# Sixteen-bit index rows for layer 1 of a four-layer graph network

## The chip, the cores and the metric

The kernel runs on one core of a Trainium2 chip. The metric is the device time of one execution in microseconds (us), given as the median over several executions. The profile is one further execution, recorded by the hardware profiler.

The engines are named as in the profile: PE multiplies matrices (PEld is its weight load), DVE is the vector engine, ACT the scalar engine, POOL the GpSimd engine, and SP the engine that issues most of the DMAs. A "q" behind a name (SPq, PEq) is that engine's instruction queue. Each engine runs its instructions in the order of its own queue, and waits on semaphores for the others.

## The reference

There are 12500 nodes with 32 features and 400000 edges. `src` is random and `dst` is sorted. Four graph layers follow each other, each with a residual and a layer norm:

```python
edge_index = jnp.stack([src, dst])
x = _layernorm(x + _L0_gnn_ref(x, edge_index, edge_weight1, edge_attr_3, edge_attr_5, L0_gnn_W), axis=-1)
x = _layernorm(x + _L1_gnn_ref(x, edge_attr_2, L1_gnn_weight, edge_index), axis=-1)
x = _layernorm(x + _L2_gnn_ref(x, edge_index, edge_attr_2, ...), axis=-1)
x = _layernorm(x + _L3_gnn_ref(x, edge_weight, edge_attr_3, edge_index, ...), axis=-1)
```

The change touches layer 1 alone. There the features are gathered at `edge_index[1]` (dst, sorted) and summed at `edge_index[0]` (src, random):

```python
def _L1_gnn_ref(x, edge_attr, weight, edge_index):   # weight: 4 x 4 x 32 x 32
    bu = _tent_basis(edge_attr[:, 0], k1)            # 4 hat functions each
    bv = _tent_basis(edge_attr[:, 1], k2)
    basis = (bu[:, :, None] * bv[:, None, :]).reshape(-1, k1 * k2)
    xj = x[edge_index[1]]
    w2 = weight.reshape(k1 * k2, f_in, f_out)
    msg = basis[:, 0:1] * (xj @ w2[0])
    for k in range(1, k1 * k2):
        msg = msg + basis[:, k:k + 1] * (xj @ w2[k])
    return jax.ops.segment_sum(msg, edge_index[0], num_segments=n_nodes)
```

## The kernel before

The edges are cut into tiles of 128. Five tiles (T = 5) make a group of 640 edges (SE), 25 groups (G) make a turn, and there are 25 turns (NG). Each layer is a hardware loop of five bodies, and each body holds five turns written out (U = 5), which is 125 groups. So a layer has 625 groups. Between two bodies all engines meet at a barrier.

The kernel is written in a framework that puts in the semaphores itself and also decides, when the program is built, in which order each engine gets its instructions. A planner walks through the program with a cost of its own for each instruction and each transfer, and gives an engine what is ready by that reckoning, the earlier in the source first. The order on an engine is therefore not always that of the source, and it is fixed before the program runs.

**The prologue** (L110 to L202) computes index tables. For layer 1 it loads `dst` as `t_i` (L169, 125 partitions of 25 x 128 integers), finds the even node below each tile's lowest target (`even`, L173 to L176), subtracts it (`rel_p`, L179) and writes the difference as 32-bit floats to the DRAM array `rel_d` (L182). Then it writes `mw_d` (L187) and reads it back as a row (`mw_row`, L189), from which two flags follow (L191 to L195). The pool that holds these tiles is given back after that, and the following constants (L260 on) use its space.

**Layer 1** (`turn1`, L685) works on a table `y_d` that holds, for every pair of nodes, the products with all 16 weight matrices. A group does this:

- SP loads four things: `bas` (L702, the 16 basis values of 640 edges, each spread over 8 partitions), `rel` (L709, the 640 differences of `rel_d`, the same row in all 128 partitions), five pieces of the table `yw` (L726, their addresses come from a register that SP loads), and `row` (L744, the 640 source indices, again the same row in all partitions). `bas`, `rel` and `row` have three buffers each.
- ACT copies `rel` into PSUM as `rel_p` (L711). This PSUM tile has one buffer.
- DVE compares `rel_p` with the node number that a partition stands for and multiplies by `bas`, in two halves `bm[:, h]` (L714).
- PE multiplies `bm` with `yw` into `pe` (L732), and ACT copies this out as `msg` (L740).
- DVE compares `row` with the sources along the partitions (`same`, L746), finds duplicates (`dup`, `later`, `to_f`, L750 to L756) and computes the rows to write to (`to`, L758).
- PE multiplies `msg` with `same` into `pm` (L762), which sums edges that share a source, and ACT copies this out as `add` (L764). `add` and `to` have four buffers.
- POOL issues five indirect DMAs (L766) which add the rows of `add` to five arrays `sums` in DRAM, at the rows in `to`.

The other layers (L0, L2, L3: `edge_pass`, L328) gather with indirect DMAs on POOL and add in SBUF. They do not use `rel_d` or the source rows.

Of the kernel before, what the change touches and what calls it, by code (L numbers as in the profile page):

```python
# [9 lines left out]

F32 = mybir.dt.float32
I32 = mybir.dt.int32
AF = mybir.ActivationFunctionType
ALU = mybir.AluOpType
AX = mybir.AxisListType
# [5 lines left out]
P = 128  # L21
F = 32
T = 5
# [16 lines left out]
def kernel(  # L40
# [25 lines left out]
    nc = tc.nc  # L66
    N = x_in.shape[0]
# [8 lines left out]
    dram = ctx.enter_context(tc.tile_pool(name="dram", bufs=1, space=DRAM))  # L76
# [81 lines left out]
    NT = NG * GT  # L158
    NM = N // 2
    PT, RT = split(NT)  # L160
    rel_d = dram.tile([NT * P], F32, name="rel_d")
    pair_d = dram.tile([NT], I32, name="pair_d")
    over_i = const.tile([1, 1], I32, name="over_i")
    more_i = const.tile([1, NG], I32, name="more_i")
# [1 line left out]
    with tc.tile_pool(name="pre1", bufs=1) as pre:  # L166
        mw_d = dram.tile([NT], F32, name="mw_d")
        t_i = pre.tile([PT, RT, P], I32, name="t_i")
        nc.sync.dma_start(t_i, dst_n.rearrange("(q r e) -> q r e", r=RT, e=P))  # L169
        pair = pre.tile([PT, RT], I32, name="pair")  # L170
        even = pre.tile([PT, RT], I32, name="even")
        top = pre.tile([PT, RT], I32, name="top")
        nc.vector.tensor_reduce(even, t_i, AX.X, ALU.min)  # L173
        nc.vector.tensor_reduce(top, t_i, AX.X, ALU.max)
        nc.vector.tensor_scalar(pair, even, 1, None, op0=ALU.logical_shift_right)
        nc.vector.tensor_scalar(even, pair, 1, None, op0=ALU.logical_shift_left)  # L176
        nc.sync.dma_start(pair_d.rearrange("(q r) -> q r", r=RT), pair)
        rel_p = pre.tile([PT, RT, P], F32, name="rel_p")
        nc.vector.tensor_tensor(  # L179
            rel_p, t_i, even[:, :, None].to_broadcast([PT, RT, P]), ALU.subtract  # L180
        )
        nc.sync.dma_start(rel_d.rearrange("(q r e) -> q r e", r=RT, e=P), rel_p)  # L182
        nc.vector.tensor_tensor(top, top, even, ALU.subtract)
        nc.vector.tensor_scalar(top, top, int(math.log2(V)), None, op0=ALU.logical_shift_right)
        mw = pre.tile([PT, RT], F32, name="mw")
        nc.vector.tensor_copy(mw, top)
        nc.sync.dma_start(mw_d.rearrange("(q r) -> q r", r=RT), mw)  # L187
        mw_row = pre.tile([1, NG, GT], F32, name="mw_row")
        nc.sync.dma_start(mw_row, mw_d.rearrange("(a n g) -> a n g", a=1, g=GT))  # L189
        more = pre.tile([1, NG], F32, name="more")  # L190
        nc.vector.tensor_reduce(more, mw_row, AX.X, ALU.max)  # L191
        over = pre.tile([1, 1], F32, name="over")
        nc.vector.tensor_reduce(over, more, AX.X, ALU.max)
        nc.vector.tensor_scalar(over_i, over, 1.0, None, op0=ALU.min)
        nc.vector.tensor_scalar(more_i, more, 1.0, None, op0=ALU.max)  # L195
        pid = pre.tile([P, 1], I32, name="pid")
        nc.gpsimd.iota(pid, pattern=[[0, 1]], base=0, channel_multiplier=1)
        nc.vector.tensor_scalar(pid, pid, 4, None, op0=ALU.logical_shift_right)
        for h in range(2):
            nc.vector.tensor_scalar(  # L200
                nid[:, h : h + 1], pid, 2.0, float(h), op0=ALU.mult, op1=ALU.add
            )  # L202
# [352 lines left out]
    with ExitStack() as sums_es:  # L555
      acc0 = sums_of(sums_es, 0, 124, 2)
      with ExitStack() as es:
        pools = layer_pools(es, 0)
        io, work = pools[:2]
# [113 lines left out]
    with ExitStack() as es:  # L673
        io = es.enter_context(tc.tile_pool(name="io1", bufs=2))
        one = es.enter_context(tc.tile_pool(name="one1", bufs=1))
        work = es.enter_context(tc.tile_pool(name="work1", bufs=2))
# [8 lines left out]
        def turn1(i, pairs, ids):  # L685
            src_f = ps_s.tile([P, G, T], F32, name="src_f")
            nc.vector.tensor_copy(
                src_f.rearrange("p g t -> p (g t)"), src_all[:, ds(i, 1), :].rearrange("p a g -> p (a g)")
            )
            spare = io.tile([P, G, T], F32, name="spare")  # L690
            nc.vector.tensor_tensor(
                spare, past[:, None, :].to_broadcast([P, G, T]), src_f, ALU.subtract
            )
            for s in range(G):
                e0 = i * (G * SE) + s * SE

                def spread(of):
                    return of[ds(e0, SE)].rearrange("(a e) -> a e", a=1).to_broadcast([P, SE])


                bas = work.tile([P, T, P], F32, name="bas", bufs=3)
                nc.sync.dma_start(  # L702
                    bas,
                    basis_d[ds(i, 1), :, s * T : (s + 1) * T, :]
                    .rearrange("a k t e -> a k (t e)")
                    .to_broadcast([8, 16, SE]),
                )
                rel = work.tile([P, T, P], F32, name="rel", bufs=3)
                nc.sync.dma_start(rel.rearrange("p t e -> p (t e)"), spread(rel_d))  # L709
                rel_p = ps_r.tile([P, T, P], F32, name="rel_p")  # L710
                nc.scalar.copy(rel_p, rel)  # L711
                bm = work.tile([P, 2, T, P], F32, name="bm")
                for h in range(2):
                    nc.vector.scalar_tensor_tensor(  # L714
                        bm[:, h], rel_p, ids[:, h : h + 1], bas, op0=ALU.is_equal, op1=ALU.mult
                    )
                yw = work.tile([P, T, 2 * F], F32, name="yw", bufs=4)
                for t in range(T):
                    at = nc.values_load(
                        pairs[0:1, s * T + t : s * T + t + 1],  # L720
                        engines=[SP],
                        min_val=0,
                        max_val=NM,
                        skip_runtime_bounds_check_because="a target's pair or N / 2, by a min below",
                    )
                    nc.sync.dma_start(  # L726
                        yw[:, t, :], y_d[ds(at, 8)].rearrange("m k f -> (m k) f")
                    )
                pe = ps_e.tile([P, T, F], F32, name="pe")
                for t in range(T):  # L730
                    for h in range(2):
                        nc.tensor.matmul(  # L732
                            pe[:, t, :],
                            bm[:, h, t, :],
                            yw[:, t, h * F : (h + 1) * F],
                            start=(h == 0),
                            stop=(h == 1),
                        )
                msg = work.tile([P, T, F], F32, name="msg", bufs=3)
                nc.scalar.copy(msg, pe)  # L740


                row = work.tile([P, T, P], I32, name="row", bufs=3)
                nc.sync.dma_start(row.rearrange("p t e -> p (t e)"), spread(src_n))  # L744
                same = work.tile([P, T, P], F32, name="same", bufs=3)
                nc.vector.tensor_tensor(  # L746
                    same, row, src_f[:, s, :, None].to_broadcast([P, T, P]), ALU.is_equal
                )
                dup = work.tile([P, T, P], F32, name="dup")
                nc.vector.tensor_tensor(  # L750
                    dup, same, before_p[:, None, :].to_broadcast([P, T, P]), ALU.mult
                )
                later = work.tile([P, T], F32, name="later")
                nc.vector.tensor_reduce(later, dup, AX.X, ALU.max)
                to_f = work.tile([P, T], F32, name="to_f")
                nc.vector.tensor_tensor(to_f, later, spare[:, s, :], ALU.mult)  # L756
                to = work.tile([P, T], I32, name="to", bufs=4)
                nc.vector.tensor_tensor(to, to_f, src_f[:, s, :], ALU.add)  # L758

                pm = ps_m.tile([P, T, F], F32, name="pm")  # L760
                for t in range(T):
                    nc.tensor.matmul(pm[:, t, :], same[:, t, :], msg[:, t, :], start=True, stop=True)  # L762
                add = work.tile([P, T, F], F32, name="add", bufs=4)
                nc.scalar.copy(add, pm)  # L764
                for t in range(T):
                    nc.gpsimd.indirect_dma_start(  # L766
                        out=sums[t],
                        out_offset=bass.IndirectOffsetOnAxis(ap=to[:, t : t + 1], axis=0),
                        in_=add[:, t, :],
                        in_offset=None,  # L770
                        compute_op=ALU.add,
                    )
# [36 lines left out]
    with ExitStack() as sums_es:  # L809
      acc2 = sums_of(sums_es, 2, 97, 1)  # L810
      with ExitStack() as es:
        pools = layer_pools(es, 2)
        io, work = pools[:2]
# [43 lines left out]
    with ExitStack() as sums_es:  # L857
      acc3 = sums_of(sums_es, 3, 80, 1)
      with ExitStack() as es:
        pools = layer_pools(es, 3, agg_bufs=1, x_bufs=0)  # L860
        io, work = pools[:2]
# [251 lines left out]
```

## Time and profile before

| what | value |
|---|---|
| median of 3 runs | 20443.71 us (20440.81 to 20443.82) |
| the profiled execution | 20448.74 us, span 20447.0 us |
| layer 1, first load to last scatter | 4483.4 to 10598.6 us of the span |
| in 4484 to 10590 us: PE, DVE, ACT, POOL busy | 4390.8, 2690.6, 739.4, 4855.7 of 6106.0 us |
| DMA in the same stretch | 16 engines busy 0.70 of the time, 127 GB/s |
| loads of a group | `bas`, `rel`, `row` 320 KB each, `yw` five of 32 KB |
| granted PE clock in layer 1 | 0.50 |

How to read it. A line of the timeline has the start in us, the duration in us, the engine, the source line, the operation, "output <- input", how many instructions were merged (x), and in brackets how long the engine had been idle and what released it. A line of the waits has who waited for whom, the total in us, the number of times and the longest. "issue" means that the engine waited for nothing that the profile shows.

### The profile page before, as it was taken

What the parts mean: (1) busy time and instruction counts of PE and PEld (TensorE: products, weight loads), DVE (VectorE), ACT (ScalarE), POOL (GpSimd) and SP (SyncE); (2) the same over time, 40 slices, a digit from 0 to 9 for tenths busy, and PEclk for the clock granted to TensorE, in tenths of its full rate; (3) what the DMA queues carried; (4) which work ended last, traced back from release to release, by engine and by line L of the source; (5) the groups of instructions that cost most, each with busy time, mean ns of one, the idle gap of its engine ahead of it and who ended that gap; (6) DMA issues with size and microseconds to landing.
All of it is one profiled execution on the core that took longest, in us unless ns stands there. A gap on an engine that the chain in (4) does not pass through costs nothing. (4 is left out here: it accounts for less than half of the span.)

```text
span 20447.0 us, 197484 instructions
## 1 busy us (share of the span) xinstructions
PE 12719.0 (62%) x51816; PEld 9979.2 (49%) x51817; DVE 10310.0 (50%) x18014; ACT 3851.0 (19%) x9168; POOL 13886.4 (68%) x12511
## 2 busy tenths in 40 slices
PE   5676676777767676776752222222467676767676
PEld 5666666656666666666652222222423333333333
DVE  3333333324444444444442222222289999999998
ACT  0000000011111111111100000000044444444443
POOL 5777777718878787887867777777555555555554
PEclk9555555555555555555555555555566666666665
DMA  1111111137767676776750000000011111111111
GB/s 39 24 25 24 23 25 24 22 104 129 129 123 129 122 129 119 132 129 122 129 106 14 15 14 14 15 13 14 10 36 31 32 31 32 31 31 32 30 31 26
DMA packets 1764667, 1156.67 MB, mean 57 GB/s; under 512 B 1103399, under 2 KB 1511663, under 8 KB 1758192
## 3 DMA queue, kind: packets, MB, share of 16 engines
q1 hardware_dynamic: 1013443, 937.43, 18.4%
q0 software_dynamic: 750000, 205.60, 11.4%
q8 instruction: 441, 7.23, 0.2%
q14 instruction: 783, 6.41, 0.1%
HBM read 1024.87 MB, written 116.94 MB: 56 GB/s over the span
## 5 line engine op out<-in xcount | busy, mean ns | idle before, releaser
L354 POOL DMA_INDIRECT xg<-x,src x6250 | 6014.2, 962 | 3691.3 <-issue 1418.3
L378 PE MATMUL agg<-hot,prod 128*124 128x64 f32 (+1 forms) x18750 | 3871.3, 399 | 3939.0 <-DVE prod L843 2822.9
L766 POOL DMA_INDIRECT sums<-add,to x3125 | 4863.0, 1556 | 1620.8 <-issue 1073.4
L378 PEld LDWEIGHTS agg<-hot,prod 128*124 128x124 f32 (+1 forms) x18750 | 3687.1, 309 | 4125.4 <-issue 4048.9
L732 PE MATMUL pe<-yw,bm 128*128 128x32 f32 x12500 | 2926.0, 403 | 1452.5 <-DVE bm L714 1349.0
L959 PE MATMUL pr<-wr,h 64*128 64x512 f32 x6250 | 3128.9, 1030 | 1104.7 <-ACT pr L954 1042.2
L354 POOL DMA_INDIRECT xg<-in_x_in,src x3125 | 3007.8, 962 | 1064.1 <-issue 810.4
L732 PEld LDWEIGHTS pe<-yw,bm 128*128 128x128 f32 x12500 | 2757.9, 329 | 1622.1 <-DVE bm L714 1489.5
L714 DVE SCALAR_TENSOR_TENSOR bm<-rel_p,nid,bas 128x640 f32<-128x640 f32 x1250 | 1090.1, 881 | 3250.8 <-ACT rel_p L711 3245.6
L959 PEld LDWEIGHTS pr<-wr,h 64*128 64x128 f32 x6250 | 1078.3, 305 | 2511.0 <-ACT pr L954 1578.8
L396 DVE TENSOR_TENSOR acc<-acc,agg 124x128 f32 (+2 forms) x1875 | 446.8, 238 | 3190.2 <-PE agg L378 3181.8
L974 DVE TENSOR_TENSOR big<-pr,fa 128x1024 f32<-128x1024 f32 x1875 | 1845.7, 1039 | 396.7 <-ACT fa L946 395.5
L954 ACT COPY pr<-b2r 128x1024 f32<-128x1024 f32 x1875 | 1594.1, 872 | 1011.8 <-DVE big L974 991.7
L985 DVE TENSOR_REDUCE red<-big 128x160 f32<-128x2560 f32 x625 | 1756.9, 2811 | 0.0
L403 ACT COPY xp<-xg 128x160 f32<-128x160 f32 x1250 | 370.0, 296 | 7272.1 <-DMA xg<-x,src 3659.9
L762 PE MATMUL pm<-msg,same 128*128 128x32 f32 x6250 | 1464.7, 403 | 272.0 <-ACT msg L740 272.0
L762 PEld LDWEIGHTS pm<-msg,same 128*128 128x128 f32 x6250 | 1380.5, 329 | 356.2 <-ACT msg L740 356.2
L843 DVE TENSOR_TENSOR prod<-gauss,xp 128x480 f32<-128x480 f32 x625 | 408.5, 654 | 1775.5 <-ACT xp L403 1749.9
L378 PEld LDWEIGHTS agg<-hot,msg 128*80 128x80 f32 x6250 | 685.2, 199 | 1260.5 <-issue 670.9
L378 PE MATMUL agg<-hot,msg 128*80 128x64 f32 x6250 | 768.9, 290 | 532.0 <-DVE acc L396 438.5
L366 DVE TENSOR_TENSOR hot<-consts,rel 128x320 f32<-128x320 f32 x1875 | 901.8, 483 | 0.0
L740 ACT COPY msg<-pe 128x160 f32<-128x160 f32 x625 | 182.5, 292 | 3734.7 <-PE pe L732 3734.7
(167 smaller groups left out, 7558.3 us busy)
## 6 DMA issues: line engine op xcount, KB each, us to landing
bas<-basis_d SPq DMA_DIRECT2D x625, 320.0 KB
rel<-rel_d SPq DMA_DIRECT2D x625, 320.0 KB
row<-in_src_n SPq DMA_DIRECT2D x625, 320.0 KB
yw<-y_d SPq DMA_DIRECT2D x3125, 32.0 KB
xg<-x,src POOLq DMA_INDIRECT x6250
dist<-in_ew_n SPq DMA_DIRECT2D x625, 96.0 KB
xg<-in_x_in,src POOLq DMA_INDIRECT x3125
sums<-add,to POOLq DMA_INDIRECT x3125
```

What stands on the lines that cost most here:

```text
L354: nc.gpsimd.indirect_dma_start(out=xg[:, t, :], out_offset=None, in_=x_dram[layer], in_offset=bass.IndirectOffsetOnAxis(ap=src[:, s * T + ...
L366: nc.vector.tensor_tensor(hot, iota_w[:, None, :].to_broadcast([P, T, W]), begun[1][:, s, :, None].to_broadcast([P, T, W]), ALU.is_equal,)
L378: nc.tensor.matmul(agg[:, c, :], prod[:, t, a:b], hot[:, t, :], start=(t == 0), stop=(t == T - 1),)
L396: nc.vector.tensor_tensor(cols, cols, agg, ALU.add)
L714: nc.vector.scalar_tensor_tensor(bm[:, h], rel_p, ids[:, h : h + 1], bas, op0=ALU.is_equal, op1=ALU.mult)
L732: nc.tensor.matmul(pe[:, t, :], bm[:, h, t, :], yw[:, t, h * F : (h + 1) * F], start=(h == 0), stop=(h == 1),)
L762: nc.tensor.matmul(pm[:, t, :], same[:, t, :], msg[:, t, :], start=True, stop=True)
L766: nc.gpsimd.indirect_dma_start(out=sums[t], out_offset=bass.IndirectOffsetOnAxis(ap=to[:, t : t + 1], axis=0), in_=add[:, t, :], in_offset ...
L954: nc.scalar.copy(pr[:, : b - a, :], b2r.rearrange("p o u j -> p (o u j)")[:, None, :].to_broadcast([P, b - a, 512]),)
L959: nc.tensor.matmul(pr[:, k, :], h[64 * k : 64 * k + 64, a // 2, :], wr[64 * k : 64 * k + 64].rearrange("h o u j -> h (o u j)"), start=Fals ...
L974: nc.vector.tensor_tensor(big[:, a * 4 : b * 4], pr[:, : b - a, :].rearrange("p t (o u j) -> p (t o) u j", u=8, j=16), fa[:, a * 4 : b * 4 ...
L985: nc.vector.tensor_reduce(red.rearrange("p t o u -> p (t o) u"), big, AX.X, ALU.add)
```

## The change

`rel_d` becomes an array of 16-bit integers. A second array of 16-bit integers, `src_d`, is added. The prologue fills it: it loads `src` (125 partitions), converts it on DVE and writes it to DRAM. In layer 1 the tiles `rel` and `row` become 16-bit integers and are loaded from the two arrays, so that each of these loads has 160 KB in place of 320 KB. `rel_p` in PSUM, `same` and everything behind them stay 32-bit floats. No loop, buffer count or instruction of layer 1 is added or removed.

```diff
-    rel_d = dram.tile([NT * P], F32, name="rel_d")
+    assert N < 1 << 15
+    rel_d = dram.tile([NT * P], I16, name="rel_d")
+    src_d = dram.tile([NT * P], I16, name="src_d")
...
-        rel_p = pre.tile([PT, RT, P], F32, name="rel_p")
+        rel_p = pre.tile([PT, RT, P], I16, name="rel_p")
         nc.vector.tensor_tensor(
             rel_p, t_i, even[:, :, None].to_broadcast([PT, RT, P]), ALU.subtract
         )
         nc.sync.dma_start(rel_d.rearrange("(q r e) -> q r e", r=RT, e=P), rel_p)
+        s_i = pre.tile([PT, RT, P], I32, name="s_i")
+        nc.sync.dma_start(s_i, src_n.rearrange("(q r e) -> q r e", r=RT, e=P))
+        s_h = pre.tile([PT, RT, P], I16, name="s_h")
+        nc.vector.tensor_copy(s_h, s_i)
+        nc.sync.dma_start(src_d.rearrange("(q r e) -> q r e", r=RT, e=P), s_h)
...
-                rel = work.tile([P, T, P], F32, name="rel", bufs=3)
+                rel = work.tile([P, T, P], I16, name="rel", bufs=3)
                 nc.sync.dma_start(rel.rearrange("p t e -> p (t e)"), spread(rel_d))
                 rel_p = ps_r.tile([P, T, P], F32, name="rel_p")
                 nc.scalar.copy(rel_p, rel)
...
-                row = work.tile([P, T, P], I32, name="row", bufs=3)
-                nc.sync.dma_start(row.rearrange("p t e -> p (t e)"), spread(src_n))
+                row = work.tile([P, T, P], I16, name="row", bufs=3)
+                nc.sync.dma_start(row.rearrange("p t e -> p (t e)"), spread(src_d))
                 same = work.tile([P, T, P], F32, name="same", bufs=3)
                 nc.vector.tensor_tensor(
                     same, row, src_f[:, s, :, None].to_broadcast([P, T, P]), ALU.is_equal
```

More of the change, by code (lines that the diff above doesn't have):

```diff
@@ L12 @@
 I32 = mybir.dt.int32
+I16 = mybir.dt.int16
 AF = mybir.ActivationFunctionType
```

## The prediction

> **What bounds layer 1 now.** I read first the windows over layer 1: no engine is full (POOL 4855.7 of 6106 us, PE 4390.8, DMA 0.70). So something goes round. The waits of layer 1 (who, for whom, total us, times, longest) say who waits in every group:
>
> ```profile
> ACT msg L740 <- PE pe L732: 3734.7, 625, 6.1
> DVE bm L714 <- ACT rel_p L711: 3245.6, 624, 7.9
> POOL sums L766 <- issue: 1072.2, 2961, 2.6
> ACT add L764 <- DMA sums<-add,to: 761.5, 313, 2.4
> ACT add L764 <- PE pm L762: 759.1, 312, 2.4
> ...
> ACT rel_p L711 <- DMA yw<-y_d: 94.4, 4, 26.0
> ```
>
> No wait for `rel`, `row` or `bas` comes 625 times: the loads are on time. DVE waits for ACT's copy `rel_p`, ACT for PE. The timeline of one group shows the ring:
>
> ```profile
> 7005.99 0.29 ACT L764 COPY add<-pm 128x160 f32<-128x160 f32 x1 [2.43 <-PE pm L762]
> 7006.17 0.70 ACT L711 COPY rel_p<-rel 128x640 f32<-128x640 f32 x1
> ...
> 7006.91 0.88 DVE L714 SCALAR_TENSOR_TENSOR bm<-rel_p,nid,bas 128x640 f32<-128x640 f32 x1 [5.20 <-ACT rel_p L711]
> 7007.71 0.15 DVE L758 TENSOR_TENSOR to<-to_f,src_f 128x5 int32<-128x5 f32 x1
> 7007.78 0.88 DVE L714 SCALAR_TENSOR_TENSOR bm<-rel_p,nid,bas 128x640 f32<-128x640 f32 x1
> ...
> 7008.57 0.81 DVE L746 TENSOR_TENSOR same<-row,src_f 128x640 f32<-128x640 int32 x1
> 7008.59 1.55 POOL L766 DMA_INDIRECT sums<-add,to  x1 [0.59 <-issue]
> ...
> 7008.71 4.05 PE L732 MATMUL pe<-yw,bm 128*128 128x32 f32 x18 [0.23 <-DVE bm L714]
> ...
> 7010.45 1.56 POOL L766 DMA_INDIRECT sums<-add,to  x1 [0.30 <-issue]
> ...
> 7012.85 0.29 ACT L740 COPY msg<-pe 128x160 f32<-128x160 f32 x1 [5.97 <-PE pe L732]
> 7013.19 2.34 PE L762 MATMUL pm<-msg,same 128*128 128x32 f32 x10 [0.44 <-ACT msg L740]
> ...
> 7015.57 0.29 ACT L764 COPY add<-pm 128x160 f32<-128x160 f32 x1 [2.43 <-DMA sums<-add,to]
> 7015.76 0.70 ACT L711 COPY rel_p<-rel 128x640 f32<-128x640 f32 x1
> ```
>
> From `rel_p` to `rel_p` it is 9.59 us: 0.74 to the first `bm`, 1.80 for both halves, 4.14 for `pe`, 0.34 to `pm`, 2.38 for `pm`, 0.19 to the next `rel_p`. The next `rel_p` needs only `rel` (loaded long before) and its PSUM buffer, free when `bm` ends at 7008.66. It runs 7.1 us later only because it stands behind `msg` and `add` in ACT's queue. Over the trace this order and this period hold in all 620 places inside the bodies. 9.59 x 625 = 5994 us, and four barriers of 25.7 us more make the 6.1 ms of layer 1.
>
> The second limit is close. POOL needs 5 x (1.556 + 0.304) = 9.30 us per group; in four of five gaps it waits 0.30 us, its least, and in the first gap longer, 0.73 us after `to` has ended. (The release of `add` by the scatter, in half of the groups, coincides with the end of `pm`; the start is 0.04 us after `pm` in both kinds.)
>
> **Edits with one answer.** `same` (L746) ends at 7009.38 and is needed at 7013.19: 3.8 us of cover, so a change of its 810 ns by half either way costs nothing; without the cover 0.4 us would be 253 us in all. The trace has no 16-bit operand on DVE, but `same` (integer in) and `dup` (all floats) take 810 and 821 ns. The Trainium skill (VectorE: DVE Perf Modes, section "What auto-detection actually checks") says that a two-source operation gets its faster mode only if every tensor is 16 bits wide, and here two are not; by it, 810 ns stays.
>
> Smaller packets: three loads and five pieces per group share 16 engines at 0.70. The 2560-byte packets take 119 ns in the middle and the 256-byte ones 18, so 16 packets per engine at about 65 ns in place of 119 free 0.9 us per group. None of that is on the ring; it is hidden by three buffers, some 20 us of lead.
>
> Starts of bodies: nothing hides the loads there. `rel` is issued at 5708.51 and `rel_p` starts at 5714.36. Eight packets per engine, each shorter by 50 to 65 ns, give 0.5 us, five times: -2.5 us (between 0 and -5).
>
> **The prologue.** Added: a load like `t_i` (issued 42.69, used at 56.79: 14 us), a conversion like L179 (3.5 us on DVE), a store half as long as that of `rel_d`. That store took the queue from 68.05 to 81.50, since `mw_row` waited behind it: 13.4 us; halved 6.7 each. If the planner issues `s_i` behind `t_i`, it lands at about 71, `rel_d` is out at 77.5, `src_d` at 84, `mw_row` lands 2 us later: +3 us against the 83.54 of L191. If `s_i` is issued only behind `rel_d`: 74, 88, conversion 91.5, store 98.5, `mw_row` 100.5: +17 us. If `src_d` goes out behind `mw_row`: -4 us. Queued behind DVE's conversion are `top` and `mw`, and behind those SP's `mw_d` and all constants from L260 on; the first gather of layer 0 waits for them, so it shifts everything one to one. I take +3, since free loads are issued early elsewhere in this prologue.
>
> **The order on ACT.** This decides. The order is the planner's, by readiness in its own reckoning, and the profile shows that the size of loads enters into it:
>
> ```profile
> 5.90 0.73 SPq L141 DMA_DIRECT2D dst_all<-in_dst_t  x1
> ...
> 32.24 0.27 SPq L134 DMA_DIRECT2D low_d<-low  x1
> 32.57 0.33 SPq L135 DMA_DIRECT2D win_d<-win  x1
> 32.94 0.34 SPq L209 DMA_DIRECT2D wc<-in_w  x1
> ```
>
> L141 overtakes L134: not source order. L209 depends on nothing, yet comes behind L134: the planner held SP or the DMAs as busy with three 1.6 MB loads until then. In layer 1 the planner gave ACT `add` before the next `rel_p`, although `rel_p` asks only for a free buffer and a landed `rel`; with `rel` landed it would have been ready first, during `pe`. So in its reckoning `rel` lands late. On the other side `to` stands behind the first half of the next `bm`, so there `rel` lands just in time for that: late by little. Between `row` and the next `rel` to land stand `bas` and `rel`, 640 KB; now 480. Per group 1120 KB become 800. If bytes are what the planner counts, `rel_p` moves ahead of `add` or `msg`. If it counts pieces or packets, of which there are as many as before, nothing moves. I hold the first for somewhat likelier.
>
> Ahead of `add`, `rel_p` runs inside ACT's 2.4 us of idle time, and ahead of `msg` inside the 6.0 us. The ring is then cut: what is late next is PE, 4.68 + 2.34 + 0.4 = 7.4 us, and before it POOL with 9.30. Counted over the trace, POOL's gaps inside the bodies exceed 0.304 us by 179 us in all. Of this 39 us are 42 gaps over 0.7 us, such as one of 1.26 at 7066.80 that POOL then caught up in ten back-to-back scatters; those stay. The gain is 140 us, at most 179, at least 100 if only part of the groups is reordered or more scatters wait.
>
> **The sum**, against the profiled execution (20448.7, which is 5.0 above the median): 20448.7 - 140 - 2.5 + 3 - 5 = **20304 us**; own range 20262 to 20350.
>
> **Rivals.** *The order stays* (0.32): the ring is untouched, 20448.7 - 2.5 + 3 - 5 = 20444; 20435 to 20465 with the bounds of the prologue. For it: no engine of the ring waits for a load, and piece counts are unchanged.
>
> *ACT reads 16-bit integers more slowly* (slower, 0.18): `rel_p` is a member of the ring, so each added ns costs 0.625 us; from 66 ns on it is over 41 us. No ACT row has an integer input. The nearest conversion is DVE's L687, integer to float, 292 ns for 125 wide, against L343, float to float, 221: 71 ns, or 44 us: 20488. From below: at 128x160 the copies take 292 and at 128x640 702 ns, 0.85 ns per element, with nothing left to gain from narrower reads unless the element rate rises. I take 0 for the sum, as this slope is the same from PSUM and SBUF. The Trainium skill (ScalarE: Activation LUTs, section "ACT is a hardware spline evaluator") gives 0.833 ns per element for fp32 and bf16 alike; it does not name integers, and by it the sum stays. Cutting the ring would hide this too, so it decides only with the old order.
>
> *The change doesn't do what it says*: node numbers below 12500 and differences fit 16 bits, and no engine converts in the loads; I give it nothing.
>
> **How the numbers follow.** Faster by over 0.2% (41 us, about what a measurement of this kernel can tell from no change) is the reordered case, 0.50; within is the old order, 0.32; slower is the slow copy, or an order with one more link in the ring, 0.18. The range runs from 20255 to 20490: all of the second case, nearly all of the first, and the price of the third's nearest row.
>
> **What would show it.** Right: in layer 1 ACT's queue has `rel_p` ahead of `add` or `msg`; the wait of `bm` for `rel_p` falls from 3245 us to a few hundred; POOL's gaps are 0.30 throughout and a body takes 1197 us in place of 1224.9; `add` waits for scatters alone. DMA share falls to about 0.6 either way. Wrong: ACT's order is still `msg`, `add`, `rel_p`, at 9.59 us; then only the prologue and five starts differ. Also wrong if `rel_p` is longer than 702 ns, or scatters grow longer than 1.556 us.

## The result and the profile after

The changed kernel takes 20450.56 us (median of 12 runs, 20445.81 to 20454.75); the kernel before, on the same chip, 20445.86 us (12 runs). The ratio is 1.0002, with a 95% interval of 0.9993 to 1.0011. That is no change, and not the forecast 20304 us: the first rival, *the order stays*, is what happened. The profiled execution took 20454.59 us.

The loads did become smaller. The windows over layer 1 (us, then the busy time of PE, PEld, DVE, ACT and POOL with the number of instructions, the granted clock, the DMA share and GB/s), first of the kernel before, then of the changed one:

```profile
4484.00:10600.00 6116.00, 4390.75 (x18750) 4138.42 (x18750) 2690.55 (x4423) 739.44 (x1875) 4863.02 (x3125) 0.50 0.70 126
```

```profile
4484.00:10600.00 6116.00, 4391.37 (x18750) 4139.05 (x18750) 2633.22 (x4424) 740.31 (x1875) 4857.87 (x3122) 0.50 0.60 93
```

PE, ACT and POOL are busy as before; DVE is not a limit at 2633 of 6116 us. The DMA share falls from 0.70 to 0.60, and nothing has come of it. The waits of layer 1 say why:

```profile
ACT msg L748 <- PE pe L740: 3734.7, 625, 6.0
DVE bm L722 <- ACT rel_p L719: 3306.4, 621, 7.7
...
ACT add L772 <- PE pm L770: 1226.0, 504, 2.4
...
ACT add L772 <- DMA sums<-add,to: 291.9, 120, 2.4
```

The ring is the same. `msg` waits for `pe` for 3734.7 us, to the tenth what it was, and `bm` waits for `rel_p` in 621 groups. The release of `add` is now put down to `pm` 504 times in place of 312. The two coincide, and it starts 2.43 us after ACT's last instruction under either name. The timeline of one group (start, duration, engine, line):

```profile
7012.33 0.29 ACT L772 COPY add<-pm 128x160 f32<-128x160 f32 x1 [2.43 <-PE pm L770]
7012.52 0.70 ACT L719 CAST rel_p<-rel 128x640 f32<-128x640 int16 x1
7013.25 0.88 DVE L722 SCALAR_TENSOR_TENSOR bm<-rel_p,nid,bas 128x640 f32<-128x640 f32 x1 [5.34 <-ACT rel_p L719]
...
7014.05 0.15 DVE L764 TENSOR_TENSOR to_f<-later,spare 128x5 f32<-128x5 f32 x1
7014.12 0.88 DVE L722 SCALAR_TENSOR_TENSOR bm<-rel_p,nid,bas 128x640 f32<-128x640 f32 x1
...
7014.92 0.15 DVE L766 TENSOR_TENSOR to<-to_f,src_f 128x5 int32<-128x5 f32 x1
7014.98 0.81 DVE L754 TENSOR_TENSOR same<-row,src_f 128x640 f32<-128x640 int16 x1
...
7019.19 0.29 ACT L748 COPY msg<-pe 128x160 f32<-128x160 f32 x1 [5.98 <-PE pe L740]
...
7021.92 0.29 ACT L772 COPY add<-pm 128x160 f32<-128x160 f32 x1 [2.43 <-DMA sums<-add,to]
7022.11 0.70 ACT L719 CAST rel_p<-rel 128x640 f32<-128x640 int16 x1
```

ACT's order is still `msg`, `add`, `rel_p`, and from `rel_p` to `rel_p` it is 7022.11 - 7012.52 = 9.59 us (median over the trace 9.593, before 9.587). ACT reads the 16-bit integers in the same 702 ns, and `same` takes the same 0.81 us. One thing has moved, and on DVE: `to_f` now stands where `to` stood, between the two halves of `bm`, and `to` behind them. This holds in 600 of the 620 groups inside the bodies; at the other 20, where a turn starts, `to` stands where `spare` stood (a DVE instruction of 128x125 at the start of a turn). It agrees with a planner that reckons with an earlier `rel`: what waits for it has moved up by one place on DVE, and by none on ACT.

What differs besides is small. The prologue, first the counterpart of L199 in the kernel before, then the changed kernel:

```profile
83.54 3.40 DVE L191 TENSOR_REDUCE more<-mw_row 1x25 f32<-1x3125 f32 x1 [15.51 <-DMA mw_row<-mw_d]
```

```profile
68.79 1.83 DVE L189 CAST s_h<-s_i 125x3200 int16<-125x3200 int32 x1 [4.70 <-DMA s_i<-in_src_n]
...
70.64 0.28 SPq L190 DMA_DIRECT2D src_d<-s_h  x1
70.74 3.49 DVE L182 TENSOR_TENSOR rel_p<-t_i,even 125x3200 int16<-125x3200 int32 x1
...
74.26 0.26 SPq L185 DMA_DIRECT2D rel_d<-rel_p  x1
...
84.89 0.22 SPq L197 DMA_DIRECT2D mw_row<-mw_d  x1
86.83 3.40 DVE L199 TENSOR_REDUCE more<-mw_row 1x25 f32<-1x3125 f32 x1 [12.07 <-DMA mw_row<-mw_d]
```

DVE waits 4.70 us for `s_i` and converts for 1.83, which puts `rel_d` at 74.26, 6.7 us later than before. From there to `mw_row` it is 10.6 us, where it was 14.0 (67.53 to 81.50). Together L199 starts 3.3 us after its counterpart, and so does the first gather (120.44 against 117.12).

In layer 1 the five starts of bodies are shorter: from the issue of the first `rel` to the first `rel_p` it is 5.34 us in the mean, where it was 6.03 (in the first body 5.41 against 5.99). This is lost again at once. From that `rel_p` to the first scatter of the body it is 12.8 us, where it was 11.9, since `to` now stands behind both halves of the next `bm`. The median period is 0.006 us longer, since `to_f` between the halves holds the second one 5 ns longer than `to` did. At the 20 turn starts it is the other way round (halves 0.867 us apart with `to`, 0.992 with `spare`), so that the mean period grows by 0.001 us only, from 9.591 to 9.592.

### The profile page after: what moved, and what is told of

Same layout as the page of the kernel before. It is cut to its first block, busy times and chain, and to the rows that moved or that the text cites. A ratio compares the mean times of both kernels' runs of the same rounds, so it can differ in the third digit from the quotient of the medians.

```text
span 20452.9 us, 197488 instructions
## 1 busy us (share of the span) xinstructions
PE 12713.7 (62%) x51816; PEld 9974.7 (49%) x51817; DVE 10253.5 (50%) x18015; ACT 3852.0 (19%) x9168; POOL 13913.8 (68%) x12511
## 3 DMA queue, kind: packets, MB, share of 16 engines
q0 software_dynamic: 750000, 205.60, 11.9%
## 5 line engine op out<-in xcount | busy, mean ns | idle before, releaser
L748 ACT COPY msg<-pe 128x160 f32<-128x160 f32 x625 | 182.8, 293 | 3734.7 <-PE pe L740 3734.7
```

## The experiments

In the expectations, theory A says that the built order of ACT and DVE sets the time of layer 1. Each expectation names what it is set against. The runs were made on three chips. The first four and the last two ran where the kernel before takes 20446 to 20449 us; the four between on a chip where it takes 22369 us, and where layer 1, the subject here, keeps its times. The time of a body is taken from its first `rel_p` to that of the next, in four places. With DVE and ACT in the order of the kernel before, bodies take 1223.7 to 1225.0 us there and 1223.9 to 1224.9 here.

**The load of `rel` ahead of that of `bas`, 32 bits wide.** In the kernel before, two statements change places, and no byte less is loaded:

```diff
+                rel = work.tile([P, T, P], F32, name="rel", bufs=3)
+                nc.sync.dma_start(rel.rearrange("p t e -> p (t e)"), spread(rel_d))
                 bas = work.tile([P, T, P], F32, name="bas", bufs=3)
...
-                rel = work.tile([P, T, P], F32, name="rel", bufs=3)
-                nc.sync.dma_start(rel.rearrange("p t e -> p (t e)"), spread(rel_d))
                 rel_p = ps_r.tile([P, T, P], F32, name="rel_p")
```

> The kernel before with 32-bit rows; the load of rel stands ahead of the load of bas in the source, nothing else. ACT's queue then has rel_p between msg and add in 115 of 125 places of a body instead of behind add. Theory A (the ring through ACT's queue sets the period, bytes do not): the ring is cut, POOL is next with 9.30 us a group, the wait of bm for rel_p falls from 3245 us to below 1000, the time falls by 100 to 179 us, to about 20305 (ratio 0.993). Theory B (the period is set by the adding scatters, for whose landing add is seen to wait in half of the groups): within 20 us of before, period 9.59.

Measured: 20261.0 us, ratio 0.9908 (0.9892 to 0.9925), 188 us less. The order that the planner builds for ACT is `msg`, `rel_p`, `add` nearly throughout: in 115 of the 125 groups of a body. The waits of its layer 1:

```profile
ACT add L764 <- DMA sums<-add,to: 4004.0, 549, 11.1
...
DVE bm L714 <- ACT rel_p L711: 273.9, 184, 7.6
```

and two groups of its timeline:

```profile
7008.87 0.29 ACT L764 COPY add<-pm 128x160 f32<-128x160 f32 x1 [7.86 <-DMA sums<-add,to]
...
7009.06 0.30 ACT L740 COPY msg<-pe 128x160 f32<-128x160 f32 x1
7009.24 0.72 ACT L711 COPY rel_p<-rel 128x640 f32<-128x640 f32 x1
...
7017.12 0.29 ACT L764 COPY add<-pm 128x160 f32<-128x160 f32 x1 [7.16 <-DMA sums<-add,to]
```

`add` now waits for a free buffer, that is for POOL's scatters, in 549 groups, and `bm` hardly waits. POOL is the bound: its gaps beyond 0.304 us inside the bodies add up to 0.7 us, where they were 179. A body takes 1187.1 us. This is what the prediction said a cut ring would look like, down to which wait ends last; the 188 us lie above the 100 to 179 us that were expected, which is taken up below.

**The same exchange in the changed kernel.** The same edit, with `rel` 16 bits wide.

> The changed kernel (16-bit rows) with the load of rel ahead of that of bas in the source. rel_p stands between msg and add in every place of ACT's queue. Theory A: like the same swap with 32-bit rows, plus some 5 us for the longer prologue: about 20310. Theory C (once the ring is cut, the DMA bytes count): at least 20 us faster than the 32-bit swap. Theory B: about 20450.

Measured: 20269.08 us, ratio 0.9912 (0.9895 to 0.9928), bodies of 1187.2 to 1188.0 us. With the ring cut, 16-bit rows bring nothing more than 32-bit ones do, and theory C (at least 20 us faster) fails. The intervals of the two overlap, and 3.5 us of the 8 between the medians are the prologue (first gather 120.98 against 117.46).

**Another way to the same order.** In the kernel before, `bas`, `rel` and `rel_p` of the next group are written ahead of `msg`:

```diff
-            for s in range(G):
+            def front(s):
                 e0 = i * (G * SE) + s * SE
...
+                return bas, rel_p
+
+            ahead = front(0)
+            for s in range(G):
...
+                if s + 1 < G:
+                    ahead = front(s + 1)
                 msg = work.tile([P, T, F], F32, name="msg", bufs=3)
```

> The kernel before with 32-bit rows; bas, rel and rel_p of the next group stand ahead of msg of this group in the source, within a turn. In 115 of 125 places of a body ACT's queue has rel_p between msg and add, and DVE's order is another one than in the swap. Theory A: as the swap, 20305 within 40 us, so that it is the place of rel_p that counts and not the order of the loads. Theory B: within 20 us of before.

Measured: 20276.64 us, ratio 0.9916 (0.9900 to 0.9933), bodies of 1189.0 to 1190.2 us, and POOL's gaps beyond 0.304 us again 0.7 us. The order on ACT is again `msg`, `rel_p`, `add`, in 115 of the 125 groups of a body. So the gain does not need `rel` ahead of `bas` on SP.

**More bytes.** In the kernel before, a second load of the source row is added, whose tile nothing reads:

```diff
                 nc.sync.dma_start(row.rearrange("p t e -> p (t e)"), spread(src_n))
+                row2 = work.tile([P, T, P], I32, name="row2", bufs=3)
+                nc.sync.dma_start(row2.rearrange("p t e -> p (t e)"), spread(src_n))
```

> The kernel before with one more load of 320 KB per group (the source row once more, into a tile that nothing reads); ACT's order is unchanged. It doubles what the change takes away. Theory A: bytes are hidden by three buffers, the DMA share rises from 0.70 to about 0.85 and the time stays within 40 us of 20446. Theory D (the loads are close to the bound, so that fewer bytes should have helped): slower by over 100 us, with waits for rel or row in many groups.

Measured: 20391.44 us, ratio 0.9972 (0.9961 to 0.9983). With 320 KB more per group, a DMA share of 0.85 and 161 GB/s, the kernel is 58 us *faster*, which no theory had expected: it lies outside the 40 us of theory A, and on the other side than theory D. Its timeline:

```profile
7009.32 0.17 DVE L758 TENSOR_TENSOR to_f<-later,spare 128x5 f32<-128x5 f32 x1
...
7009.60 0.16 DVE L760 TENSOR_TENSOR to<-to_f,src_f 128x5 int32<-128x5 f32 x1
...
7013.96 0.70 ACT L711 COPY rel_p<-rel 128x640 f32<-128x640 f32 x1
...
7014.69 1.68 DVE L714 SCALAR_TENSOR_TENSOR bm<-rel_p,nid,bas 128x640 f32<-128x640 f32 x2 [4.94 <-ACT rel_p L711]
```

ACT's order is the old one. On DVE, `to` has gone ahead of the next `bm`, whose halves now follow each other directly (printed as one line, x2) 0.801 us apart, where it was 0.867. The period is 9.520 us. 0.067 x 620 is 42 us. Five bodies of 1213.8 us in the mean, in place of 1224.5, make 54 us, so that some 12 us lie at the starts and ends of the bodies.

**That order alone.** To tell the place of `to` from anything else that the added load may do, `bm` is held behind the `to` of the group before, and nothing else changes:

```diff
-                for h in range(2):
-                    nc.vector.scalar_tensor_tensor(
+                with tc.issue_after(to_ins.ins) if s else ExitStack():
+                    for h in range(2):
+                        nc.vector.scalar_tensor_tensor(
...
-                nc.vector.tensor_tensor(to, to_f, src_f[:, s, :], ALU.add)
+                to_ins = nc.vector.tensor_tensor(to, to_f, src_f[:, s, :], ALU.add)
```

> The kernel before with 32-bit rows; DVE must issue both halves of bm behind to of the group before, so that to no longer stands between the two halves. ACT's order stays msg, add, rel_p, and no load is added. Theory A (what stands between the halves of bm is a link of the ring and costs about 0.07 us per group, and the gain of the kernel with the extra load came from this order alone): period 9.52 instead of 9.59, 45 to 60 us faster, about 20392. Theory E (the extra load itself, or its effect on the DMA queues, gave that gain): within 15 us of before.

Measured: 22326.09 us against 22369.16, ratio 0.9981 (0.9972 to 0.9991): 43 us less, with the period at 9.520 us and the halves 0.801 us apart. That is just below the expected 45 to 60 us, and 15 us less than the added load gave. The bodies (1213.7 to 1214.9 us) explain some 4 us of the 15: at the 20 turn starts `spare` still stands between the halves here. The rest is not in the bodies of layer 1; single runs of the kernel before differ by 35 us on this chip. So the place of `to` gives most of the gain of the kernel with the added load, and theory E (within 15 us of before) fails. The same in the changed kernel:

> The changed kernel (16-bit rows) with both halves of bm behind to of the group before, so that neither to_f nor to stands between them. Theory A: 45 to 60 us faster than the changed kernel, some 5 us slower than the same order with 32-bit rows (longer prologue): about 20397. If bytes mattered in this order, it would be faster than the 32-bit kernel of this order.

Measured: 22319.83 us, ratio 0.9976 (0.9966 to 0.9985), period 9.520 us, bodies of 1213.2 to 1213.7 us. Held in one order, the narrow and the wide kernel have the same median period to the nanosecond. The median time is 6 us below that of the wide one, where 5 us more had been expected. The two intervals overlap, and the runs of either spread over 19 to 31 us. Of the traces, 1.0 us for each body speaks for the narrow one: half of it comes from the turn starts (`to` between the halves in place of `spare`), half from the stretch between two bodies, which itself varies by 1 us. So bytes may be worth a few us here, not more.

**The exchanged loads with the old order on ACT.** In the changed kernel with exchanged loads, `rel_p` is held behind `add` within a turn:

```diff
-                nc.scalar.copy(rel_p, rel)
+                with tc.issue_after(add_ins.ins) if s else ExitStack():
+                    nc.scalar.copy(rel_p, rel)
...
-                nc.scalar.copy(add, pm)
+                add_ins = nc.scalar.copy(add, pm)
```

> The changed kernel with the load of rel ahead of that of bas as in swap16, but rel_p is held behind add in ACT's queue. Theory A (the gain of the swap is ACT's order alone): period 9.59 again, about 20450, within 20 us of the changed kernel. Theory F (the earlier issue of the load of rel gave the gain): about 20265 as swap16.

Measured: 22326.23 us, ratio 0.9981 (0.9972 to 0.9991), 43 us less than the kernel before, so the expected agreement with the changed kernel was missed. The trace has the reason: the first group of a turn is not held (`if s`), and at the 20 turn starts inside the bodies `rel_p` did slip ahead of `add`. There a period of 6.87 us is followed by one of 9.77; 2 x 9.593 - 6.87 - 9.77 is 2.5 us, and 20 of them 51 us, of the 52 us by which the five bodies are shorter (1214.1 us in the mean). In the held places the period is 9.593 us again. So the exchange of the loads shows no gain where ACT's order is held.

**Only the source row 16 bits wide** (one execution; the changed kernel with `rel_d`, the prologue's `rel_p` and `rel` back at 32 bits):

```diff
-    rel_d = dram.tile([NT * P], I16, name="rel_d")
+    rel_d = dram.tile([NT * P], F32, name="rel_d")
...
-                rel = work.tile([P, T, P], I16, name="rel", bufs=3)
+                rel = work.tile([P, T, P], F32, name="rel", bufs=3)
```

> Half of the change: only the source rows are 16-bit integers, rel_d and rel stay 32-bit floats. Theory A: DVE's order is that of before (to between the halves of bm), so it is the load of rel that moved to_f in the changed kernel; period 9.59. The prologue now writes rel_d in full (13.4 us) and src_d (6.7 us) in one queue, so the first gather moves from 117.1 to about 127 us (120.4 in the changed kernel); the time is 20450 to 20465.

Measured: 22382.16 us, beside 22369.16 for the kernel before; one execution can't tell 13 us there, where those of the kernel before lie between 22349.88 and 22384.91. Its trace decides: period 9.587 us, halves 0.867 apart, DVE's order as in the kernel before. So in the changed kernel it is the narrower `rel` that moved `to_f`; a narrower `row` alone moves neither DVE's order nor ACT's. The prologue pays for the wide store: the first gather is at 126.19.

**Fewer bytes ahead of `rel`, the loads in their old places.** If the planner reckons when `rel` lands from the bytes that stand between `row` and it, then a narrower `bas` must do what the exchange did. In the changed kernel the basis values too become 16-bit floats:

```diff
-    basis_d = dram.tile([NG, 16, GT, P], F32, name="basis_d")
+    basis_d = dram.tile([NG, 16, GT, P], BF16, name="basis_d")
...
-                bs = work.tile([P, 4, P], F32, name="bs", bufs=2)
+                bs = work.tile([P, 4, P], BF16, name="bs", bufs=2)
...
-                bas = work.tile([P, T, P], F32, name="bas", bufs=3)
+                bas = work.tile([P, T, P], BF16, name="bas", bufs=3)
```

> The changed kernel with the basis values too as 16-bit floats in DRAM and in the tile bas (the computation differs by this rounding). Theory A (the planner reckons when rel lands from the bytes that stand ahead of it, and the change took too few of them away): between row and the landing of the next rel it was 640 KB in the kernel before, 480 in the changed one, and is 320 here; the order built for ACT is msg, rel_p, add in 115 of the 124 places looked at. So the time falls to that of the version with the loads exchanged, 0.991 to 0.992 of the kernel before, bodies of 1186 to 1191 us, add waits for the scatters, POOL's gaps 0.30. bm stays near 877 ns, since only one of its two tensor inputs is 16 bits wide. Rival G (it is the place of the load in the source that counts, and bytes never pay): the period stays 9.59 us and the ratio 1.000, give or take 0.001. Rival H (the order helps, but a 16-bit bas makes bm slower): bm above 900 ns, ratio above 0.993.

Measured: 20254.24 us, ratio 0.9907 (0.9891 to 0.9924), bodies of 1185.1 to 1186.5 us. Its layer 1:

```profile
ACT add L773 <- DMA sums<-add,to: 4210.2, 537, 9.0
...
DVE bm L723 <- ACT rel_p L720: 545.9, 164, 7.7
```

`bm` takes 876 ns in the mean, and POOL's gaps beyond 0.304 us add up to 0.8 us. So rivals G and H fail. This and the exchanged loads are the fastest versions of the study, within their intervals of each other; the exchange loads every byte at full width.

The same edit in the kernel before, with `rel` and `row` at 32 bits, makes the bytes between `row` and the landing of `rel` the 480 KB of the changed kernel:

> The kernel before with the basis values alone as 16-bit floats (the computation differs by this rounding); rel and row stay 32 bits wide. Between row and the landing of the next rel it is 480 KB, as in the changed kernel. Theory A (bytes ahead of rel): the same order as the changed kernel on both engines, ACT msg, add, rel_p at 9.59 us and DVE with to_f between the halves of bm; ratio 1.000, give or take 0.001, bodies 1223.7 to 1225.7. Rival H (a 16-bit bas changes bm): a period other than 9.59 by the difference of two bm, with the order as in the changed kernel.

Measured: 20441.41 us, ratio 0.9997 (0.9988 to 1.0007), period 9.593 us, halves of `bm` 0.872 us apart with `to_f` between them, ACT in the old order. The bodies of 1222.9 to 1223.7 us are up to 0.8 us shorter than expected, since the starts are shorter with a narrow `bas` (3.7 to 4.2 us from the issue of `rel` to `rel_p`). By narrowing a different tile it gives the changed kernel's order and period.

## Why the prediction was wrong

**What held.** Layer 1 is bound by the ring through ACT's queue; the loads are hidden; POOL's 9.30 us per group is next. Cutting the ring without a byte less gave 188 us, and the changed kernel, with the ring whole, gave nothing for a DMA share of 0.60 in place of 0.70. The edits that were costed at nothing cost nothing: `same` 0.81 us, ACT's copy 702 ns. So the slower rival, a copy 71 ns longer, fell. The grounds on both sides of it were thinner than they look: the 71 ns compare a cast into PSUM (L687) with a copy within SBUF (L343), and the 0.85 ns per element lie between a copy out of PSUM (`msg`) and one out of SBUF (`rel_p`), so that they cannot show one slope for both. On the copy, the page of the Trainium skill that the prediction cited (ScalarE: Activation LUTs, "ACT is a hardware spline evaluator") does not name integers; here 702 ns for 640 elements is what the 32-bit copy took. The two-source operation with one 16-bit input also kept its time, as the cited section of VectorE: DVE Perf Modes has it.

The prologue's +3 us was measured as +3.3, but in another sequence: `src_d` went out ahead of `rel_d`, and the conversion took 1.83 us, not 3.5. That the sum came out is in part luck. The five starts of bodies gave 0.7 us each where 0.5 had been predicted, but this did not reach the time: the new order on DVE delays the first scatter of each body by 0.9 us.

**The step that failed** is "The order on ACT". The prediction had two cases: if the planner counts bytes, `rel_p` moves ahead of `add` or `msg`; if it counts pieces, nothing moves. It held the first for likelier (0.50), and the 140 us of the sum rest on it. The orders built agree with a planner that counts bytes, and still `rel_p` did not move: the case between, fewer bytes but not few enough, was not there. The kernels bound it:

| bytes between `row` and the landing of `rel` | kernels | order on ACT | on DVE between the halves of `bm` | period or bodies |
|---|---|---|---|---|
| 960 KB, `row2` among them | `row2` added | `msg`, `add`, `rel_p` | nothing | 9.520 us |
| 640 KB | before; only `row` narrow | `msg`, `add`, `rel_p` | `to` | 9.587 us |
| 480 KB | changed; only `bas` narrow | `msg`, `add`, `rel_p` | `to_f` | 9.593 us |
| 320 KB | changed with narrow `bas`; loads exchanged, wide | `msg`, `rel_p`, `add` | `later`; `to_f` | bodies 1185 to 1187 us |
| 160 KB | loads exchanged, narrow | `msg`, `rel_p`, `add` | `later` | bodies 1187 to 1188 us |

(The version with `bas`, `rel` and `rel_p` written ahead of `msg` is not in the table: there the load of `rel` stands ahead of that `row`.) The more bytes stand ahead, the later the planner puts what depends on `rel`; the order on ACT turns between 480 and 320 KB. It is not the sum of a group's bytes: only `row` narrow and only `bas` narrow both load 960 KB per group and have different orders. Nor is it the number of loads, which narrowing leaves as it was. "Late by little" was the error: `to` behind the first half of `bm` showed that `rel` was just in time *there*, and said nothing of how far it was from `add`. Where between the two sizes it turns, and by what formula, is open; no run changed the planner's own costs.

**A term that was mis-sized.** For the cut ring the prediction kept 39 us of gaps over 0.7 us as POOL's own, and took 140 us of 179. There are no such gaps in the kernels with the ring cut: POOL's excess fell from 179 us to 0.7. The gaps were waits of the ring, too. The 188 us are even above the upper bound of 179; the rest lies at the starts and ends of the bodies (1224.5 - 1187.1 = 37.4 us for each, of which POOL's gaps inside account for 35.6).

**A link that was overlooked.** The prediction put 1.80 us for both halves into the ring without asking what stands between them. It is a DVE operation of 128x5 that costs 0.067 us per group there, 42 us in all. That alone is as much as the prediction's bound of "no change" (41 us), and it is most of the 58 us by which 320 KB more made the kernel faster.

## What to carry to other kernels

Find the ring before the bytes are cut: where no engine is full and no wait for a load comes in every group, look at which instruction stands behind which in one queue, and try the order itself first. An argument from a scheduler's order gives a direction, not a distance: that a load lands "late" in its reckoning does not say how much smaller it must be for the order to turn, and this calls for a low chance or a second size. A change of sizes in such a framework is also a change of order, so compare the orders of both kernels, engine by engine, before a difference is put down to bytes.

## What the runs showed of the hardware

In the changed kernel ACT converts 128x640 16-bit integers to floats in 702 ns, as long as it copied floats before (with the ring cut 708 ns in the mean for floats, 710 to 712 for integers). DVE's conversion of 125x3200 integers from 32 to 16 bits took 1.83 us, about half of the 3.49 of a subtraction of that size.

A packet of half the bytes takes more than half the time. From 6000 to 9000 us a packet of 2560 bytes took 119 ns in the middle before and 113 after, and one of 1280 bytes took 78; the prediction had estimated about 65.

A granted clock of 1.00 in a profile can mean that none was recorded. Two kernels with `to` ahead of `bm`, on one chip, from 7000 to 10000 us (the wide one, then the narrow one):

```profile
7000.00:10000.00 3000.00, 2177.35 (x9297) 2052.20 (x9296) 1360.95 (x2196) 367.18 (x930) 2412.59 (x1550) 0.50 0.71 128
```

```profile
7000.00:10000.00 3000.00, 2178.80 (x9308) 2053.60 (x9308) 1362.14 (x2199) 366.84 (x930) 2412.77 (x1551) 1.00 0.61 94
```

The lines give a clock of 0.50 and of 1.00, and yet PE is busy for 234 ns per matmul in both (2177.35 / 9297 and 2178.80 / 9308), and the period is 9.520 us in both. It does not follow that the clock is of no account here. The trace of the wide kernel has a record of 0.50 from 1880 to 16601 us of the span; that of the narrow one has no record of the clock at all ahead of 16601 us. Which clock it was granted in layer 1 is open.

One chip took 9% longer than the others (22369 against 20446 us for the kernel before), all of it outside layer 1: the first `rel_p` came at 5572 to 5584 us in place of 4490. The instructions of layer 0 are as long there as elsewhere (from 120 to 4000 us a gather on POOL 959 ns in the wide kernel with `to` ahead of `bm`, 963 in the kernel before), but DVE is idle for 5.8 us ahead of each addition to `acc` (L396; 2749.9 us at 473 of them), where it was 3.2 (1927.2 at 605). Why is open; no run was made for it.
